# Right column halves of the first four row tiles by seven 256-column products, and a reordered dequantization, in a two-layer kernel on one core

## The chip, the cores and the metric

The kernel runs on one core of a Trainium2 chip. The time is the device time of one execution in microseconds (us); of several runs the median is given. The engines are TensorE (PE in the profile; its weight loads are PEld), VectorE (DVE), ScalarE (ACT), GpSimd (POOL) and SyncE (SP, which here only issues transfers). Each takes the instructions of its own queue in order and waits at an instruction until the semaphores that it needs have come.

## The reference

The input x has 2048 rows of 1024 (4 x 512). Two layers follow each other, each with a residual and a layer norm:

```python
attn = einsum('ds,td->st', w1, w2) * sparse_mask       # 1024 x 1024, nonzero near the diagonal
y = einsum('bds,st->bdt', x, attn) + b2
x = layernorm(x + gelu(y))

w = take_along_axis(lut4, idx, axis=1)   # 1024 x 1024; idx from 4 bit planes, 32 codes to an int32
x = layernorm(x + x @ w.T + bias)        # rows with a norm above 64 would use 8 bits
```

All of it is float32. In the data no row's norm exceeds the limit and the mask is zero outside its band; the kernel counts exceptions as it goes, and only if there were any would it run a general path.

## The kernel before

Rows are worked in 16 tiles of 128 (`NT`), features in 8 blocks of 128 (`KT`); `HALF` is 512 columns, which is one bank of TensorE's accumulators.

**Preparation.** `w2` is transposed block by block on TensorE, and the product with `w1` gives the band of `attn`, row block by row block (L454). VectorE multiplies each by its mask and so empties the bank (L476). Beside that the second layer's weight is dequantized (`dequantize_pair`). A pair is two blocks of 128 output features. Eight VectorE instructions (L297) spread the bits of the pair's codes into the tile `v`, of which there is one buffer. Each block has two sides. Each side has four entries, each a table value chosen by bit 0: three on ScalarE (L322) into one triple tile `e` (three buffers), one on GpSimd (L326) into `root`. VectorE's predicated copies (L329 to L331) choose between them by bits 1 and 2, and a last one (L335) between the sides by bit 3. The finished block is transposed on TensorE, and ScalarE copies it into `wT`. `steps(1)` in the code releases one further side of it after each row block and after some row tiles. The row tiles 2 to 11 are loaded when the preparation's memory is free, that is after the last L476.

**First layer.** `attention(n)` fills a bank pair with the bias (ScalarE, L526), adds ten matmuls (L532), takes the Gelu into `z` (two buffers), adds the residual with its row sum `total` (VectorE, L561), and calls `stats`. `stats` makes the negative mean `nm` (VectorE, L377), the sum of squares about it by a Square on ScalarE (L380), and on GpSimd the factor `r` (L382, L383). `normalize` (L387) is put off to a list, `later`, and issued by the next `now()`, after some of the following work.

**Second layer, row tiles 0 to 3 (`EARLY`).** The rows are transposed on TensorE into the tiles `kept`. Each tile has a left half of 512 columns, worked among the attentions 4 to 7, and a right half, worked among the attentions 12 to 15 (`SOON` is 12). A half is eight matmuls of 512 columns (L575) and one VectorE instruction that adds the bias and sums the row (`combine`, L587). After each right half comes one of the four weight sums (`weight_sum`, L636) that the pairs need.

**Second layer, row tiles 4 to 15, in pairs.** `ffn_pair` computes the two-by-two block product of a pair of row tiles in seven products of four matmuls of 512 columns instead of eight (L692). It needs four sums of weight blocks, t1 to t4, made once, and four of row blocks, s1 to s4, made for each pair (`pair_inputs`; s1 and s3 on VectorE L675, L676, s2 and s4 on GpSimd L678, L679). Its rows come transposed through memory: a VectorE transpose of 32 x 32 squares (`squares`, L642), a store to `there`, and four loads into `rows`. Three banks (u, v, w) hold partial products; VectorE reads u and w between products (L705, L709, L712), and a bank that is added to again must have been read first. The last row tile is finished in quarters (L762).

**Order of the work.** A scheduler orders each engine's queue, by its own estimates of when an instruction can start. From attention 8 on (`manual_schedule`) the VectorE queue has the order of the program instead. The outputs of the tiles 0 to 3 go through a tile `o` with one buffer.

Of the kernel before, what the change touches and what calls it, by code (L numbers as in the profile page):

```python
# [192 lines left out]
def kernel(  # L193
# [21 lines left out]
    with ExitStack() as main:  # L215
# [77 lines left out]
        def dequantize_pair(pair):  # L293

            v = dq.tile([P, 2 * B_L, 8, WORDS], I32, tag="v", name="v", bufs=1)
# [9 lines left out]
            bits = v.rearrange("o a s w -> o a (s w)").bitcast(U8)  # L305
            for t in range(2):
# [6 lines left out]
                for side in range(2):  # L313
                    e = dq.tile([P, 3, D], FP, tag="e", name="e", bufs=3)
                    root = dq.tile([P, D], FP, tag="root", name="root", bufs=4)
                    roots.append(root)
                    entry = [root, e[:, 0, :], e[:, 1, :], e[:, 2, :]]
# [14 lines left out]
                    if side == 0:  # L332
                        yield
# [19 lines left out]
        def dequantize_all():  # L353
            for pair in range(KT // 2):
                if pair == 1:
                    tc.keep_in_program_order(differences(2, KT))
                yield from dequantize_pair(pair)
# [7 lines left out]
        differences(0, 2)  # L365
        low = dequantize_all()
# [6 lines left out]
        def stats(u, total):  # L373
# [3 lines left out]
            nc.vector.tensor_scalar(nm, total, -1.0 / D, None, ALU.mult)  # L377
            junk = work.tile([P, D], BF, tag="junk", name="junk", bufs=1)
            ss = work.tile([P, 1], FP, tag="ss", name="ss", bufs=4)
            nc.scalar.activation(junk, u, AF.Square, bias=nm, accum_out=ss)  # L380
            r = work.tile([P, 1], FP, tag="r", name="r", bufs=4)
            nc.gpsimd.tensor_scalar(r, ss, 1.0 / D, EPS, ALU.mult, ALU.add)  # L382
# [200 lines left out]
        sums = const.tile([P, NT, NH], FP, name="sums")  # L583

        def combine(n, h, ps, other):

            return nc.vector.scalar_tensor_tensor(  # L587
                x_tiles[n][:, ts(h, HALF)],
# [5 lines left out]
                accum_out=sums[:, n, h : h + 1],  # L594
            )

        def finish_rows(n):
            y = x_tiles[n]
            total = work.tile([P, 1], FP, tag="total", name="total", bufs=4)
            nc.vector.tensor_tensor(total, sums[:, n, 0:1], sums[:, n, 1:2], ALU.add)  # L600
# [12 lines left out]
        def ffn_half(n, xT, h):  # L613
            ps = ps_mm.tile([P, D], FP, tag="mm", name="mm")
            product(ps[:, :HALF], xT, h)
            now()
            combine(n, h, ps[:, :HALF], bias_bc[:, ts(h, HALF)])
            if h == 1:
                finish_rows(n)
# [11 lines left out]
        def weight_sum(pool, i):  # L631
# [4 lines left out]
            nc.vector.tensor_tensor(weights[i], plus, minus, ALU.subtract)  # L636
# [21 lines left out]
        def pair_inputs(pool, n, top, low):  # L658
# [6 lines left out]
            def by_squares(block):  # L665
# [5 lines left out]
                halves(f"early{2 * i + side}") for i in range(3)  # L671
# [10 lines left out]
        def ffn_pair(pool, n, blocks, between):  # L682
# [6 lines left out]

            def times(ps, a, b, start, stop):  # L690
                for k in range(KH):
                    nc.tensor.matmul(  # L692
                        out=ps,
                        lhsT=a[:, k, :],
# [147 lines left out]
        for i, (what, n) in enumerate(todo):  # L842
# [14 lines left out]
            if what == "attention":  # L857
# [4 lines left out]
                if n < 2 * EARLY:  # L862
                    now()
# [63 lines left out]
```

## Time and profile before

| | |
|---|---|
| time, three runs | 360.46 us median (358.38 to 361.06) |
| time of the profiled execution | 360.45 us |
| its span | 358.7 us |
| busy | PE 92%, PEld 57%, DVE 60%, ACT 50%, POOL 25% |
| transfers | 43.90 MB, 122 GB/s over the span |
| mean granted TensorE clock | 0.973 |
| products of 512 columns in the pair stage, eight records | 3.43 us on the chain that ended last |
| a right half (L575, sixteen records) | 6.87 us on that chain |

A matmul on float32 appears as two records. The span runs from the first to the last instruction of the profiled execution, and the time of the same execution is 1.75 us longer. Busy shares are of the span. The profile's matmul durations overlap each other, so what a series costs is read from the starts of its records or from the chain, not from the mean of one.

### The profile page before, as it was taken

To read this page: it belongs to the slowest core of one execution; us is meant where nothing else is said; L and a number is where in the kernel's file an instruction comes from. 1 tells how busy PE (TensorE), PEld (TensorE's weight loads), DVE (VectorE), ACT (ScalarE), POOL (GpSimd) and SP (SyncE) were. 2 spreads that over 40 slices of the span, in tenths; PEclk is the share of its full clock that TensorE was granted. 3 is DMA by queue.
4 is the path that set the end of the run, shared out by engine and by line. 5 is a ranking of instruction groups with operands and counts; after the bars stand their busy time and mean duration, and the time that the engine had idled before them with its cause. 6 is when DMAs were issued, how large, how long until landed. Compare 5 with 4: busy or idle time off the path is not lost.

```text
span 358.7 us, 3719 instructions
## 1 busy us (share of the span) xinstructions
PE 329.9 (92%) x1228; PEld 205.7 (57%) x1228; DVE 214.5 (60%) x341; ACT 179.4 (50%) x257; POOL 90.9 (25%) x131
## 2 busy tenths in 40 slices
PE   7799867598999999999999998999999999999990
PEld 7688756495765759966656643443444443444450
DVE  0589898546997885436476853653644535634342
ACT  3795893978958988974346311303214114024020
POOL 1630431425013442312312530401304004004010
PEclk9899998879999999999999999999999999999996
DMA  8999207700000000320264425153554450441103
GB/s 250 320 320 384 80 0 288 298 2 0 0 0 2 1 0 3 126 111 26 79 215 165 140 80 175 58 199 100 199 177 137 188 175 8 189 154 58 58 3 125
DMA packets 28475, 43.90 MB, mean 122 GB/s; under 512 B 7584, under 2 KB 20640, under 8 KB 28448
## 3 DMA queue, kind: packets, MB, share of 16 engines
q1 hardware_dynamic: 26832, 42.66, 34.9%
q10 hardware_dynamic: 1616, 0.93, 0.9%
q8 instruction: 11, 0.18, 0.2%
q14 instruction: 16, 0.13, 0.1%
HBM read 28.90 MB, written 14.68 MB: 122 GB/s over the span
## 4 chain that ended last, share of the span: by engine, by line
PE 60%; ACT 12%; DMA 11%; DVE 8%; issue 3%; POOL 2%; SPq 2%; ACTq 0%; POOLq 0%; DVEq 0%
PE u L692 15%; PE mm L532 12%; PE mm L575 12%; PE w L692 8%; ACT e L322 6%; PE pt L281 5%; PE v L692 4%; PE mm L454 4%; DMA rows<-there 3%; ACT junk L380 2%; DMA q<-in_L_ffn_qweight_dram 2%; DMA x<-in_L_attn_x_dram 2%; DMA there<-squares 1%; DMA w_sb<-in_L_attn_w_dram 1%; SPq L652 1%
## 5 line engine op out<-in xcount | busy, mean ns | idle before, releaser
L532 PE MATMUL mm<-attn,xT 128*128 128x198 f32 (+2 forms) x320 | 62.5, 353 | 6.9 <-ACT mm L526 6.9
L380 ACT ACTIVATE junk<-x,nm 128x1024 bf16<-128x1024 f32 x31 | 35.7, 1151 | 59.7 <-DVE nm L377 57.3
L532 PEld LDWEIGHTS mm<-attn,xT 128*128 128x128 f32 x320 | 54.8, 197 | 14.6 <-ACT mm L526 7.6
L322 ACT ACTIVATE e<-v,lt,diff 128x1024 f32<-128x1024 uint8 x48 | 56.8, 1243 | 12.6 <-DVE v L297 11.0
L575 PE MATMUL mm<-wT,xT 128*128 128x512 f32 x128 | 56.4, 593 | 1.0 <-ACT wT L282 1.0
L326 POOL TENSOR_SCALAR root<-v,diff,lt 128x1024 f32<-128x1024 uint8 x16 | 31.3, 1965 | 57.9 <-DVE v L297 26.2
L692 PE MATMUL u<-t,halves 128*128 128x512 f32 x96 | 43.3, 593 | 1.0 <-DVE x L712 1.0
L575 PEld LDWEIGHTS mm<-wT,xT 128*128 128x128 f32 x128 | 23.7, 190 | 28.1 <-issue 26.1
L382 POOL TENSOR_SCALAR r<-ss 128x1 f32<-128x1 f32 x31 | 10.4, 334 | 108.8 <-ACT junk L380 108.6
L674 ACT COPY halves<-rows 128x1024 f32<-128x1024 f32 x6 | 6.3, 1048 | 55.4 <-DMA rows<-there 55.4
L454 PE MATMUL mm<-w2T,w_sb 128*128 128x268 f32 (+1 forms) x128 | 30.8, 391 | 2.2 <-ACT w2T L282 2.2
L692 PEld LDWEIGHTS u<-t,halves 128*128 128x128 f32 x96 | 18.2, 190 | 24.3 <-issue 22.5
L678 POOL TENSOR_TENSOR halves<-halves 128x512 f32<-128x512 f32 x6 | 9.5, 1585 | 84.5 <-DVE halves L675 68.3
L642 DVE STREAM_TRANSPOSE squares<-x 128x1024 f32<-128x1024 f32 x12 | 24.3, 2029 | 11.0 <-DMA there<-squares 11.0
L387 DVE TENSOR_SCALAR x<-x,nm,r 128x1024 f32<-128x1024 f32 x16 | 13.0, 813 | 29.0 <-POOL r L383 29.0
L330 DVE COPY_PREDICATED root<-v,e 128x1024 f32<-128x1024 uint8 x16 | 23.3, 1457 | 8.0 <-POOL root L326 4.6
L454 PEld LDWEIGHTS mm<-w2T,w_sb 128*128 128x128 f32 x128 | 23.8, 197 | 6.2 <-ACT w2T L282 2.7
L281 PE MATMUL pt<-ident,x 128*128 128x128 f32 x160 | 21.8, 281 | 4.0 <-DVE x L387 4.0
L561 DVE SCALAR_TENSOR_TENSOR x<-z,x 128x1024 f32<-128x1024 f32 x16 | 21.4, 1335 | 6.2 <-ACT z L557 6.2
L329 DVE COPY_PREDICATED e<-v,e 128x1024 f32<-128x1024 uint8 x16 | 21.3, 1329 | 3.5 <-ACT e L322 3.5
L281 PEld LDWEIGHTS pt<-ident,x 128*128 128x128 f32 x160 | 19.4, 152 | 5.9 <-DVE x L387 4.3
L282 ACT COPY xT<-pt 128x512 f32<-128x512 f32 x40 | 21.4, 591 | 2.3 <-PE pt L281 2.3
(93 smaller groups left out, 438.5 us busy)
## 6 DMA issues: line engine op xcount, KB each, us to landing
x<-in_L_attn_x_dram SPq DMA_DIRECT2D x16, 512.0 KB, 7.4
out_dram<-o SPq DMA_DIRECT2D x14, 512.0 KB, 2.6
there<-squares SPq DMA_DIRECT2D x12, 512.0 KB, 3.1
rows<-there SPq DMA_DIRECT2D x48, 128.0 KB, 2.9
w_raw<-in_L_attn_w_dram SPq DMA_DIRECT2D x8, 512.0 KB, 6.8
w_sb<-in_L_attn_w_dram SPq DMA_DIRECT2D x3, 1024.0 KB, 6.9
w_sb<-in_L_attn_w_dram SPq DMA_DIRECT2D x2, 512.0 KB, 7.2
x<-_L_attn_sparse_mask_dram SPq DMA_DIRECT2D x2, 413.0 KB, 3.7
```

The lines of the kernel that those rows point to most:

```text
L281: nc.tensor.transpose(pt[:, j, :], block(g * (HALF // P) + j), ident)
L282: done = nc.scalar.copy(dst[:, g * (HALF // P) : (g + 1) * (HALF // P), :], pt)
L322: nc.scalar.activation(entry[j], plane(0), AF.Identity, scale=d_k, bias=l_k)
L326: nc.gpsimd.tensor_scalar(entry[j], plane(0), d_k, l_k, ALU.mult, ALU.add)
L330: nc.vector.copy_predicated(root, plane(1), entry[1])
L380: nc.scalar.activation(junk, u, AF.Square, bias=nm, accum_out=ss)
L454: part = nc.tensor.matmul(out=ps[:, : hi - lo], lhsT=w1_sb[s][:, k, :], rhs=w2T[:, k, lo:hi], start=(k == 0), stop=(k == KT - 1),)
L532: nc.tensor.matmul(out=ps[:, a:b], lhsT=xT[:, s, :], rhs=attn[:, s, a - lo : b - lo], start=False, stop=hi == D or (h == 0 and window(s + ...
L561: nc.vector.scalar_tensor_tensor(xt, z, 1.0, xt, ALU.mult, ALU.add, accum_out=total)
L575: nc.tensor.matmul(out=ps, lhsT=xT[:, k, :], rhs=wT[:, k, ts(h, HALF)], start=(k == 0), stop=(k == KT - 1),)
L642: nc.vector.transpose(out=t, in_=x_tiles[n].rearrange("t (c j k) -> t c k j", c=Q, k=KT))
L692: nc.tensor.matmul(out=ps, lhsT=a[:, k, :], rhs=b[:, k, :], start=start and k == 0, stop=stop and k == KH - 1, skip_group_check=True,)
```

## The change

**The first right halves.** The row tiles 0 to 3 are taken by twos. `early_blocks` makes the four sums of row blocks for two tiles (two on VectorE, two on GpSimd); it is called for both twos after attention 10. `right_weight_sums` makes four sums of 512 x 256 weight blocks on VectorE after attention 11. `ffn_rights` computes the two right halves in seven products of four matmuls with 256 columns; its banks u and w are taken from the transposes' banks, v from the main ones. It is called twice, ahead of attentions 12 and 14. Each row's sum now has three parts. The weight sums for the pairs stand after the attentions 12, 14 (two) and 15, and numbers 1 and 3 run on GpSimd. The first two `squares` come after the attentions 12 and 13 instead of 13 and 14.

**The dequantization.** `v` has two buffers, and a pair's bits are spread (`unpack`) in the middle of the second block of the pair before. The entries have single buffers, seven of them, instead of three triples.

**The statistics.** The Square takes the row's sum as its bias and -1024 as its scale, so that its result is larger by 1024 x 1024, which `r` and the count of exceptions take out again. `nm` is made on GpSimd.

```diff
-            v = dq.tile([P, 2 * B_L, 8, WORDS], I32, tag="v", name="v", bufs=1)
+        def unpack(pair):
+            v = dq.tile([P, 2 * B_L, 8, WORDS], I32, tag="v", name="v", bufs=2)
...
-                    e = dq.tile([P, 3, D], FP, tag="e", name="e", bufs=3)
...
-                    entry = [root, e[:, 0, :], e[:, 1, :], e[:, 2, :]]
+                    entry = [root] + [
+                        dq.tile([P, D], FP, tag="e", name="e", bufs=7) for _ in range(3)
+                    ]
...
                     if side == 0:
+                        if t == 1 and pair + 1 < KT // 2:
+                            if pair == 0:
+                                tc.keep_in_program_order(differences(2, KT))
+                            unpack(pair + 1)
                         yield
...
-            nc.vector.tensor_scalar(nm, total, -1.0 / D, None, ALU.mult)
+            nc.gpsimd.tensor_scalar(nm, total, -1.0 / D, None, ALU.mult)
...
-            nc.scalar.activation(junk, u, AF.Square, bias=nm, accum_out=ss)
+            nc.scalar.activation(junk, u, AF.Square, scale=float(-D), bias=total, accum_out=ss)
...
-            nc.gpsimd.tensor_scalar(r, ss, 1.0 / D, EPS, ALU.mult, ALU.add)
+            nc.gpsimd.tensor_scalar(r, ss, 1.0 / D**3, EPS, ALU.mult, ALU.add)
...
-            nc.vector.tensor_tensor(weights[i], plus, minus, ALU.subtract)
+            engine = nc.gpsimd if i % 2 else nc.vector
+            engine.tensor_tensor(weights[i], plus, minus, ALU.subtract)
...
+        def right_weight_sums(pool):
...
+            nc.vector.tensor_tensor(t1, r12, r11, ALU.subtract)
+            nc.vector.tensor_tensor(t2, r22, t1, ALU.subtract)
+            nc.vector.tensor_tensor(t3, r22, r12, ALU.subtract)
+            nc.vector.tensor_tensor(t4, r21, t2, ALU.subtract)
...
+        def early_blocks(pool, n):
+            a11, a12 = kept[n][:, :KH, :], kept[n][:, KH:, :]
+            a21, a22 = kept[n + 1][:, :KH, :], kept[n + 1][:, KH:, :]
...
+            nc.vector.tensor_tensor(s1, a21, a22, ALU.add)
+            nc.vector.tensor_tensor(a21, a11, a21, ALU.subtract)
+            nc.gpsimd.tensor_tensor(s2, s1, a11, ALU.subtract)
+            nc.gpsimd.tensor_tensor(s4, a12, s2, ALU.subtract)
...
+        def ffn_rights(n):
...
+            times(u, a11, r11, True, False)
+            nc.vector.tensor_tensor(y11, u, left, ALU.add)
+            times(w, s1, t1, True, False)
+            nc.vector.tensor_tensor(y22, w, right, ALU.add)
+            times(u, s2, t2, False, False)
+            nc.vector.tensor_tensor(y12, u, right, ALU.add)
+            times(w, s4, r22, False, True)
+            combine(n, 3, w, y12, R)
+            times(u, s3, t3, False, False)
+            combine(n + 1, 3, u, y22, R)
+            now()
+            times(v, a12, r21, True, True)
+            combine(n, 2, v, y11, R)
+            finish_rows(n)
+            times(u, a22, t4, False, True)
+            combine(n + 1, 2, u, left, R)
+            now()
+            finish_rows(n + 1)
...
-        for m in range(EARLY):
-            todo += [("right", m), ("attention", SOON + m)]
+        for m in range(0, EARLY, PAIR):
+            todo += [("rights", m), ("attention", SOON + m), ("attention", SOON + m + 1)]
...
-                if n >= SOON + 1:
-                    attention(n, xT, lambda: prepare_pair(EARLY, n - SOON - 1))
+                if SOON <= n <= SOON + PAIR:
+                    attention(n, xT, lambda: prepare_pair(EARLY, n - SOON))
...
+                if n == SOON - 2:
+                    for m in range(0, EARLY, PAIR):
+                        early_blocks(last, m)
+                if n == SOON - 1:
+                    now()
+                    right_weight_sums(last)
+                for i in {SOON: (1,), SOON + 2: (2, 3), SOON + 3: (4,)}.get(n, ()):
+                    weight_sum(last, i)
+            elif what == "left":
+                ffn_left(n, xT)
             else:
-                ffn_half(n, xT, 0 if what == "left" else 1)
-                if what == "right":
-                    weight_sum(last, n + 1)
-                    now()
+                ffn_rights(n)
```

## Prediction

> **What bounds the kernel now.** I read the page's engine rows first, then busy time by stretch, then TensorE's timeline.
>
> ```profile
> span 358.7 us, 3719 instructions
> PE 329.9 (92%) x1228; PEld 205.7 (57%) x1228; DVE 214.5 (60%) x341; ACT 179.4 (50%) x257; POOL 90.9 (25%) x131
> ```
>
> ```profile
> 50.70:92.50 41.80, 31.23 (x146) 25.18 (x146) 28.49 (x40) 32.13 (x43) 16.19 (x21) 0.88 0.32 126
> 92.50:149.00 56.50, 55.08 (x282) 41.04 (x281) 44.77 (x66) 48.68 (x65) 16.79 (x24) 1.00 0.00 1
> 149.00:201.50 52.50, 52.50 (x218) 35.33 (x217) 30.71 (x47) 28.03 (x42) 13.75 (x31) 1.00 0.39 134
> 201.50:227.40 25.90, 24.56 (x58) 10.50 (x57) 14.87 (x22) 4.91 (x7) 8.03 (x9) 1.00 0.35 116
> 227.40:350.30 122.90, 121.14 (x291) 54.37 (x289) 58.53 (x110) 28.88 (x59) 20.34 (x32) 1.00 0.36 126
> ```
>
> The first figure after the length of a stretch is PE's busy time. Only 50.7 to 92.5 leaves it much idle; 149.0 to 201.5, which the change rewrites, has no gap at all. TensorE is the bound, and what any other engine does counts where TensorE must wait for it. Its timeline shows those places (in brackets the wait and its releaser):
>
> ```profile
> 14.72 3.76 PE L454 MATMUL mm<-w2T,w_sb 128*128 128x268 f32 x8 [2.02 <-ACT w2T L282]
> ...
> 56.24 5.33 PE L532 MATMUL mm<-attn,xT 128*128 128x198 f32 x20 [5.49 <-ACT mm L526]
> ...
> 70.96 1.97 PE L281 MATMUL pt<-ident,x 128*128 128x128 f32 x8 [4.04 <-DVE x L387]
> ...
> 85.49 7.13 PE L575 MATMUL mm<-wT,xT 128*128 128x512 f32 x16 [1.03 <-ACT wT L282]
> ...
> 212.33 3.67 PE L692 MATMUL w<-wT,halves 128*128 128x512 f32 x8 [0.34 <-DVE x L709]
> 217.00 3.70 PE L692 MATMUL u<-t,halves 128*128 128x512 f32 x8 [1.00 <-DVE x L712]
> ...
> 249.05 3.67 PE L692 MATMUL u<-t,a 128*128 128x512 f32 x8 [0.88 <-ACT a L677]
> ```
>
> A wait also costs clock. By stretches again, PEclk third from last:
>
> ```profile
> 14.70:18.40 3.70, 3.68 (x9) 2.70 (x10) 2.12 (x3) 3.70 (x4) 3.70 (x3) 0.54 1.22 329
> 56.20:61.40 5.20, 5.16 (x20) 4.55 (x21) 5.10 (x7) 0.94 (x1) 0.00 (x0) 0.71 0.95 375
> 70.90:74.40 3.50, 3.44 (x16) 3.45 (x17) 3.50 (x6) 3.13 (x5) 0.05 (x1) 0.50 0.00 0
> ```
>
> After waits of 2.0, 5.5 and 4.0 us the clock is 0.54, 0.71 and 0.50 for some 4 us, while the waits of about 1 us kept 1.00. I charge 1.7 us (half of 3.5) after a long wait, and half of that, 0.9, after one of 2 to 3.5 us.
>
> **The change, part by part** (times on the old kernel's clock until I shift them).
>
> *Seven products instead of eight halves.* In the chain eight records (four fp32 matmuls) of 512 columns take 3.43 us and a right half, sixteen, 6.87; eight records of 256 columns (L762) take 1.73. So 4 x 6.87 = 27.5 becomes 14 x 1.72 = 24.1: -3.4 us, all on the path. Were weight loads the limit, a product could not fall below 8 x 0.19 = 1.52, so they are not; 1.72 is measured.
>
> *Bits and entries.* Eight extractions (1.72 us) of a pair move ahead of the end of the pair before. Now ScalarE waits for them three times, 11.0 us in all, the longest 6.1. In the built order the vector queue meets the second pair's first extraction at about 20.1, where the codes have not landed: SP issues them up to 17.9, landing takes 5.8, so it stands until some 23 with predicated copies and mask products behind it (TensorE needs the held product bank only at 25.5, so it doesn't wait). The bits are then ready at 33.4 instead of 37.7. ScalarE follows with entries at 1.17 us each and its copies, and its first bias copy (L526) ends at 53.2 instead of 56.1: -3. The built order then puts attentions 2 and 3 ahead of the first left product, where TensorE now waits 4.04 us for x0 and runs at half clock: 53.2, two attentions of 3.6 with their 0.87 transposes to 63, attention 2 to 66.6 (x0 is ready at 66.4), attention 3 to 71.1, transposes to 73.8. The left product needs four wT copies that stand behind a Gelu and two Squares on ScalarE: 77.3 against 85.49, -8.2; the wait of 3.5 us ahead of it costs 1.7 of clock. Net -6.5. Seven single entries instead of nine in triples hold ScalarE back only if it runs more than seven ahead; I find it there once, by less than 1 us. Bounds: 0 (the later vector queue eats it all) to -15 (all that TensorE loses between 50.7 and 85.5 in waits and slow clock); I stay at the walked value. After that the dequantization has slack: the last root is built at 137.3 and transposed at 146.2.
>
> *Square on the row's sum.* Each statistic loses nm (0.15 us on DVE and its hand-over) ahead of the Square; POOL gains 31 x 0.19 = 5.9 us beside 75% idle time. Worth about 0.25 us a chain; counted in the walk below.
>
> *The added vector and POOL work around the right products.* The vector engine follows program order from attention 8 on. New in it: four block sums of 512 (0.69 each), four weight sums of 1024 (half of L636's 2.28: 1.15 each), fourteen bank reads of 256 instead of four of 512. On POOL: s2 and s4 twice (L678 1.59, L679 1.27), and weight sums 1 and 3 of 2048. No row shows the latter: from below two one-input 1024s, 2 x 1.20 = 2.4; from above 4 x 1.59 = 6.4; nearest is 4 x 1.27 less three fixed parts of 0.19: 4.5.
>
> Where they stand decides. POOL's queue has weight sum 1 between nm and r of row tile 9, so r comes at 154.8 instead of 151.4, and normalizing x9 heads the vector queue: the residual of tile 10 moves from 153.8 to 155.6, the four block sums end at 159.4, and s2, s4 stand ahead of r of tile 10 on POOL (normalized at 161.5), again of tile 11 (167.0). The first right weight sum ends at 168.9. TensorE has the first and last products and six matmuls of attention 12 to do, until about 163, and then waits for it: +5.8 us, and 1.7 of clock. Bounds: 3 (weight sum 1 free) to 9.
>
> Second: the output tile "o" has one buffer, and two stores (2.6 us each) now follow each other instead of 11 us apart. Behind the last bank read at 182: Square and r, o(0), the store, o(1), a 1.95 stream transpose, a residual, its statistic, another transpose, another residual, 15.4 us until the second pair's first bank is read, beside 12.9 of TensorE work: +2.5 and 0.9 of clock. Third: the same two stores of the second pair, two halves, two residuals, weight sums 2 and 4 (2.28 each) stand ahead of the first 512 pair's bank read: +3.1 and 0.9. That pair loses its old waits (-1.7) and gains one of 0.9 on u, since v is used up earlier; the pair behind it has v to fill its wait: -1.0. Bounds of these two waits together: 0 to 10.
>
> Sum: -6.5 - 3.4 + 7.5 + 3.4 + 4.0 - 1.7 + 0.9 - 1.0 = +3.2, a span of 361.9. The profiled execution took 360.45 around a span of 358.7, so 1.75 is added: **363.6 us**. Its 360.45 is also the median of the runs (360.46).
>
> The Trainium skill (TensorE: Matmul & The Clock Gate, Part 1) states that the clock falls to half after an idle window of about 3.4 us. The row at 14.72 shows 0.54 after only 2.02 us. By the page alone the waits of 2.5 and 3.1 us would cost no clock and the time would be 361.8.
>
> **Rivals.**
> *The vector engine keeps up.* The first wait is only its lower bound of 3.0, without slow clock, and the other two vanish: -6.5 - 3.4 + 3.0 - 1.7 + 0.9 - 1.0 = -8.7, **351.8 us**. For it: DVE is busy only 31 of 52.5 us there. Against: it is the order, not the load, that makes it late. It decides from the point where the three waits and their clock come to less than 8 us instead of 14.9.
> *No early gain.* If the codes land later, or contention slows the predicated copies (1.2 us alone, up to 2.23 beside POOL's roots), the first left product starts as late as before and only the middle counts: 363.6 + 6.5 = **370.1**; half of it gives 366.9.
> *The products don't shrink*: 256 columns at their 379 ns record instead of 215: 112 x 0.164 = 18 us more. L762 in the chain speaks against it.
>
> **How the numbers follow.** The walk as it stands 0.43, the vector engine keeping up 0.31, no or half an early gain 0.24, no shrinking 0.02. About 1% (3.6 us) is what a measurement can tell from no change. Faster by over 1%: the second case, 0.31. The forecast lies 0.9% above the old time and splits into 0.27 within and the rest above; with the other slow cases 0.42 slower. The likeliest case has its own range, 360 to 368. The range for 8 in 10 goes from 352 to 369.5.
>
> **What would show it.** Right: the first left product near 77; TensorE waiting for a vector weight sum for about 6 us after attention 11; two waits of 2 to 4 us for vector bank reads, one before attention 15 and one in the first 512 pair; the stretch from attention 11 to the last attention longer than before although its products are shorter. Wrong: the first left product near 85; no wait of TensorE above 3 us after attention 11; r of tile 9 not behind POOL's weight sum; 256-column products of more than 1.8 us.

## The result, and the profile after

The kernel after takes **373.46 us** (median of four runs, 372.06 to 375.58) against 359.55 us before: ratio 1.0389, 95% interval 1.0321 to 1.0458. It is slower, as the likeliest case said, but by 13.9 us, not by 3: the time lies above the range. The profiled execution took 375.58 us, its span is 15.1 us longer than that of before.

The page's first rows, after:

```profile
span 373.8 us, 3831 instructions
PE 331.3 (89%) x1275; PEld 214.9 (57%) x1276; DVE 216.2 (58%) x330; ACT 178.8 (48%) x257; POOL 138.4 (37%) x168
```

TensorE is busy for about as long as before (329.9 us) in a longer span; POOL has 47 us more. Busy time by stretch, cut where the same work begins: the first left product, attention 10, the first 512 pair, the second 512 pair, the end of TensorE's work (columns as in the prediction: behind the length of the stretch PE's busy time, then that of PEld, DVE, ACT and POOL; the clock is third from last).

```profile
0.00:80.01 80.01, 65.78 (x370) 57.55 (x371) 58.17 (x92) 62.14 (x79) 38.32 (x29) 0.98 0.66 218
80.01:144.04 64.03, 62.27 (x299) 44.08 (x297) 47.24 (x55) 54.60 (x72) 34.22 (x40) 1.00 0.00 1
144.04:210.17 66.13, 55.65 (x267) 48.05 (x265) 30.07 (x52) 26.13 (x39) 28.03 (x41) 0.90 0.26 92
210.17:243.00 32.83, 26.26 (x58) 11.18 (x58) 20.44 (x22) 6.66 (x10) 11.95 (x15) 0.95 0.36 120
243.00:365.40 122.40, 121.35 (x291) 54.06 (x289) 57.96 (x104) 29.27 (x59) 25.36 (x44) 1.00 0.36 127
```

Before, the same five took 85.49, 63.48, 52.55, 25.88 and 122.90 us. So the first one gained 5.5 us, the third (which holds the rewritten right halves) lost 13.6 and the first 512 pair 7.0; the others moved by 0.5 us each. TensorE's timeline has the places:

```profile
52.94 3.86 PE L542 MATMUL mm<-attn,xT 128*128 128x198 f32 x20 [2.63 <-ACT mm L536]
71.05 1.12 PE L281 MATMUL pt<-ident,x 128*128 128x128 f32 x8 [3.35 <-DVE x L397]
80.01 7.13 PE L585 MATMUL mm<-wT,xT 128*128 128x512 f32 x16
...
165.11 3.78 PE L690 MATMUL w<-t,halves 128*128 128x256 f32 x8 [5.87 <-DVE t L667]
171.95 1.89 PE L690 MATMUL u<-t,halves 128*128 128x256 f32 x8
173.68 1.89 PE L690 MATMUL w<-wT,s 128*128 128x256 f32 x8
197.24 3.75 PE L690 MATMUL u<-t,halves 128*128 128x256 f32 x8 [4.42 <-DVE x L715]
226.32 5.15 PE L690 MATMUL u<-t,halves 128*128 128x512 f32 x8 [5.69 <-DVE x L789]
239.34 3.67 PE L690 MATMUL u<-t,a 128*128 128x512 f32 x8 [0.88 <-DVE x L598]
```

The three waits that were forecast are there, and at their places: the first right weight sum after attention 11, the second group's bank read, the first 512 pair's bank read. At full clock a 256-column product takes 1.73 us (171.95 to 173.68). Behind the first two waits it takes twice that, and the 512-column product behind the third takes 5.0 us instead of 3.43 (226.32 to 231.31). The clock in the stretches behind the three waits shows why:

```profile
165.10:172.00 6.90, 6.89 (x24) 5.83 (x25) 4.24 (x5) 1.29 (x3) 0.00 (x0) 0.55 0.00 0
197.20:203.20 6.00, 5.96 (x17) 4.91 (x18) 0.65 (x2) 3.81 (x5) 3.28 (x5) 0.60 0.40 128
226.30:231.40 5.10, 5.08 (x9) 2.35 (x10) 3.32 (x3) 0.00 (x0) 1.02 (x3) 0.71 0.23 96
```

6.9 x 0.45 + 6.0 x 0.40 + 5.1 x 0.29 = 7.0 us of clock, where 3.5 were charged. What the vector engine stood for, in its own timeline (in brackets its wait):

```profile
150.03 0.81 DVE L397 TENSOR_SCALAR x<-x,nm,r 128x1024 f32<-128x1024 f32 x1 [6.01 <-POOL r L393]
163.10 0.81 DVE L397 TENSOR_SCALAR x<-x,nm,r 128x1024 f32<-128x1024 f32 x1 [3.73 <-POOL r L393]
163.83 1.22 DVE L667 TENSOR_TENSOR t<-wT 128x1024 f32<-128x1024 f32 x1
186.72 0.81 DVE L397 TENSOR_SCALAR o<-x,nm,r 128x1024 f32<-128x1024 f32 x1 [5.24 <-DMA out_dram<-o]
212.87 0.81 DVE L397 TENSOR_SCALAR o<-x,nm,r 128x1024 f32<-128x1024 f32 x1 [2.96 <-DMA out_dram<-o]
```

and on POOL, why r of row tile 9 came late: the weight sum stands between `nm` and r.

```profile
144.11 0.22 POOL L387 TENSOR_SCALAR nm<-total 128x1 f32<-128x1 f32 x1 [1.18 <-DVE x L571]
144.52 4.54 POOL L650 TENSOR_TENSOR t<-wT 128x2048 f32<-128x2048 f32 x1 [0.19 <-issue]
149.15 0.19 POOL L392 TENSOR_SCALAR r<-ss 128x1 f32<-128x1 f32 x1
```

The waits and their clock are 5.87 + 4.42 + 5.69 + 7.0 = 23.0 us, more than the whole loss of 15.1 us of span, beside which stand the early gain and the shorter products. The vector queue in program order is full of instructions that wait for something, while the engine itself is busy 30 of the 66 us of the third stretch.

### The profile page after: what moved, and what is told of

Same layout as the page of the kernel before. It is cut to its first block, busy times and chain, and to the rows that moved or that the text cites. A ratio compares the mean times of both kernels' runs of the same rounds, so it can differ in the third digit from the quotient of the medians.

```text
span 373.8 us, 3831 instructions
## 1 busy us (share of the span) xinstructions
PE 331.3 (89%) x1275; PEld 214.9 (57%) x1276; DVE 216.2 (58%) x330; ACT 178.8 (48%) x257; POOL 138.4 (37%) x168
## 4 chain that ended last, share of the span: by engine, by line
PE 43%; DVE 19%; POOL 15%; DMA 9%; issue 5%; ACT 4%; SPq 3%; POOLq 0%; DVEq 0%; ACTq 0%
PE u L690 14%; PE w L690 8%; PE mm L585 6%; PE mm L542 6%; PE pt L281 4%; POOL root L333 4%; PE v L690 3%; DMA rows<-there 3%; DVE squares L737 3%; DVE e L336 3%; DVE root L338 2%; ACT junk L390 2%; POOL r L393 2%; DMA out_dram<-o 2%; DMA there<-squares 2%
## 5 line engine op out<-in xcount | busy, mean ns | idle before, releaser
L390 ACT ACTIVATE junk<-x,total 128x1024 bf16<-128x1024 f32 x31 | 35.7, 1152 | 77.8 <-DVE x L571 34.0
L333 POOL TENSOR_SCALAR root<-v,diff,lt 128x1024 f32<-128x1024 uint8 x16 | 49.1, 3076 | 43.0 <-DVE root L346 17.6
L690 PE MATMUL u<-t,halves 128*128 128x512 f32 (+1 forms) x112 | 50.6, 598 | 10.2 <-DVE x L789 5.7
L690 PEld LDWEIGHTS u<-t,halves 128*128 128x128 f32 x112 | 22.6, 206 | 35.9 <-issue 21.9
L387 POOL TENSOR_SCALAR nm<-total 128x1 f32<-128x1 f32 x31 | 15.5, 500 | 72.4 <-DVE x L571 33.7
L690 PE MATMUL w<-t,halves 128*128 128x512 f32 (+1 forms) x64 | 27.2, 573 | 5.9 <-DVE t L667 5.9
L464 PE MATMUL mm<-w2T,w_sb 128*128 128x268 f32 (+1 forms) x128 | 29.2, 376 | 2.9 <-ACT w2T L282 2.8
L585 PE MATMUL mm<-wT,xT 128*128 128x512 f32 x64 | 28.4, 596 | 1.8 <-DVE x L598 1.8
L337 DVE COPY_PREDICATED root<-v,e 128x1024 f32<-128x1024 uint8 x16 | 21.1, 1320 | 5.5 <-POOL root L333 5.5
L690 PEld LDWEIGHTS w<-t,halves 128*128 128x128 f32 x64 | 13.2, 208 | 18.5 <-issue 11.5
```

What stands on the lines that cost most here:

```text
L333: nc.gpsimd.tensor_scalar(entry[j], plane(0), d_k, l_k, ALU.mult, ALU.add)
L337: nc.vector.copy_predicated(root, plane(1), entry[1])
L390: nc.scalar.activation(junk, u, AF.Square, scale=float(-D), bias=total, accum_out=ss)
L464: part = nc.tensor.matmul(out=ps[:, : hi - lo], lhsT=w1_sb[s][:, k, :], rhs=w2T[:, k, lo:hi], start=(k == 0), stop=(k == KT - 1),)
L585: nc.tensor.matmul(out=ps, lhsT=xT[:, k, :], rhs=wT[:, k, ts(h, HALF)], start=(k == 0), stop=(k == KT - 1),)
L690: done = nc.tensor.matmul(out=ps, lhsT=a[:, k, :], rhs=b[:, k, :], start=start and k == 0, stop=stop and k == KH - 1, skip_group_check=True,)
```

## The experiments

Each time is beside runs of the kernel before on the same chip. "Middle" is the profiled time from the first left product to the second 512 pair, which holds all that the change lost. `e_...` names a run.

| kernel | us (median) | ratio to before, 95% | first left product | middle |
|---|---|---|---|---|
| before | 359.55 | | 85.49 | 141.9 |
| after | 373.46 | 1.0389 (1.0321-1.0458) | 80.01 | 162.8 |
| `after_again` | 373.60 | 1.0398 (1.0360-1.0436) | 79.92 | 161.3 |
| `e_old_rights` | 354.96 | 0.9892 (0.9848-0.9935) | 80.97 | 142.6 |
| `e_new_rights` | 378.77 | 1.0557 (1.0482-1.0631) | 85.45 | 160.7 |
| `e_deq_only` | 357.23 | 0.9939 (0.9916-0.9961) | 82.41 | 143.0 |
| `e_sums_first` | 370.55 | 1.0335 (1.0288-1.0381) | 79.81 | 156.7 |
| `e_sums_later` | 370.41 | 1.0297 (1.0248-1.0345) | 80.28 | 158.3 |
| `e_o_two` | 372.56 | 1.0386 (1.0337-1.0435) | 79.91 | 158.0 |
| `e_nm_vector` | 372.25 | 1.0357 (1.0320-1.0395) | 79.51 | 161.2 |
| `e_wsum_vector` | 374.24 | 1.0412 (1.0371-1.0453) | 80.05 | 162.0 |
| `e_no_sums` | 358.31 | 0.9963 (0.9932-0.9994) | 80.02 | 143.5 |
| `e_order_pool` | 370.47 | 1.0304 (1.0258-1.0350) | 81.76 | 155.1 |
| `e_order_vector` | 352.98 | 0.9822 (0.9782-0.9861) | 79.81 | 140.9 |
| `e_order_again` | 353.76 | 0.9842 (0.9805-0.9878) | 79.85 | 141.5 |
| `e_mix_blocks` | 353.59 | 0.9830 (0.9787-0.9872) | 80.21 | 141.7 |
| `e_mix_weights` | 356.04 | 0.9886 (0.9838-0.9933) | 79.84 | 144.3 |
| `e_one_o` | 359.14 | 0.9999 (0.9980-1.0018) | 79.82 | 144.0 |
| `e_lump` | 360.63 | 1.0026 (1.0005-1.0046) | 80.00 | 145.7 |
| `e_apart` | 354.53 | 0.9856 (0.9827-0.9886) | 80.54 | 139.4 |

### The parts of the change, one at a time

`e_old_rights` is before with the new dequantization and statistics; `e_new_rights` is before with everything else of the change.

> The kernel before with the new dequantization and the new statistics, but with the old right halves, two to a pair of row tiles and 512 columns wide. In the profile after, the early stretch (to the first left product) is 5.5 us shorter than before, the next stretch 0.5 longer, and the whole loss lies behind: 13.6 us from attention 10 to the first 512 pair, 7.0 in that pair. Theory A: the loss belongs to the seven products and to the order of the work that feeds them, so this kernel keeps the early gain alone: 354 to 356 us, 4 to 5.5 below before. Rival B: the loss belongs to the statistics, whose sign change now runs on POOL and there takes up to 2.2 us beside vector work: then the pairs of 512 lose here too, and the time is 361 or more.

> The kernel before with the seven products, their block and weight sums and their order, but with the old dequantization and the old statistics. Theory A: the middle and the first 512 pair lose what they lose in the kernel after, 17 to 21 us: 377 to 381 us. Rival B (the statistics on POOL are half of it): 366 to 371 us. Rival C (the two parts hurt only together): within 3 us of before.

354.96 and 378.77: theory A in both. The dequantization and the statistics together are a gain of 1.1%, and the seven products with their order of work lose 20 us by themselves, with the old statistics as well.

### Removing one suspect from the kernel after

`e_sums_first` puts the right weight sums ahead; `e_sums_later` in addition leaves out the line that normalizes tile 11 there (comment added):

```diff
                 if n == SOON - 2:
+                    right_weight_sums(last)
                     for m in range(0, EARLY, PAIR):
                         early_blocks(last, m)
                 if n == SOON - 1:
                     now()                # e_sums_later: both lines gone
-                    right_weight_sums(last)
```

> The kernel after, with the four right weight sums put ahead of the block sums, at attention 10, not behind the normalization of row tile 11. Theory: it is the order of the vector queue that makes TensorE wait 5.9 us for the first sum (it ended at 165.1, behind 3.7 us in which the vector engine waited for r of tile 11) and then run at half clock; with the sums first that wait and some 2 to 3 us of slow clock go, 6 to 9 us in all: 364.5 to 367.5. Rival: the vector engine has too much to do there, and the wait moves to the block sums or to the bank reads: less than 2 us saved.

The first wait shrank from 5.9 to 1.3 us, and the time falls by only 3 us: the next bank read is late in its place, with the same slow clock, and the third wait grew from 5.7 to 6.4. TensorE, `e_sums_first`:

```profile
155.61 1.99 PE L690 MATMUL w<-t,halves 128*128 128x256 f32 x8 [1.33 <-DVE halves L682]
167.11 3.75 PE L690 MATMUL u<-t,halves 128*128 128x256 f32 x8 [5.03 <-DVE x L715]
```

> As the run with the right weight sums first, and the normalization of row tile 11 isn't called for ahead of the first product's bank read any more, so that the vector queue doesn't wait for r of that tile there (2.3 us). With the sums first the wait for the first sum went (5.9 to 1.3 us) and one of 5.0 us came two products later, for that bank read. Theory: the vector queue's order sets each of these waits; this one falls from 5.0 to below 2 us and the time to 364 to 367. Rival (the vector engine has more to do there than TensorE whatever the order): the wait only moves on, and the time stays at 369 or more.

370.41: the rival's number, a miss for the theory. That wait fell from 5.0 to 4.3 only, because the vector engine still waited 6.0 us for r of tile 9 behind POOL's weight sum, and the sums stood behind that.

`e_o_two` lets the odd row tiles be normalized in place, so that two stores never share the buffer:

```diff
-                    o = last.tile([P, D], FP, tag="o", name="o")
+                    o = y if n % 2 else last.tile([P, D], FP, tag="o", name="o")
```

> The kernel after, but the normalized rows of tiles 1 and 3 are written in place and stored from there, so that no two stores share the one output buffer. Theory: the vector engine stood 5.24 us (tile 1) and 2.96 us (tile 3) for the store of the tile before; the second wait of TensorE (4.4 us and 2.5 of slow clock) goes, and the third (5.7 and 1.5) shrinks by about 3: 7 to 10 us in all, 363.5 to 366.5. Rival: without the stores the vector engine meets the next late thing (r of POOL, the Square) and TensorE's waits shrink by less than a third: 371 or more.

The second wait fell from 4.4 to 1.3 us and the middle by 3.4 against `after_again`, yet the ratio didn't move beyond its interval. In its profile the pairs behind the middle take 124.8 us where the kernel after has 122.4: TensorE's queue there was ordered differently, with waits of 0.4 to 1.0 us for bank reads in some of the pairs. That happened in several runs below and goes with some 2 to 3 us each time.

`e_nm_vector` puts `nm` back on the vector engine, `e_wsum_vector` the weight sums 1 and 3.

> The kernel after once more, on the same chip and against the same runs as the three kernels beside it, since the differences to it are of 1 to 8 us: 371 to 375 us. Its waits stand where they stood: for the first right weight sum 5.9 us, for the second pair's bank read 4.4, for the first 512 pair's 5.7.

> The kernel after with the sign change of the row sum back on the vector engine; the Square still takes the row's sum. Theory (order of the vector queue): the sign change on POOL costs the pairs little, since TensorE's long waits were as long in the kernel that had the old statistics with the seven products (5.5, 4.3, 5.7 us): 0 to 2 us less than after. Rival: the sign changes of 2.2 us beside the sums of the weights on the vector engine make the third wait, which falls below 3.5 us: 3 us or more less than after.

> The kernel after with weight sums 1 and 3 of the 512 pairs back on the vector engine. Theory: POOL's weight sum of 4.5 us, which its scheduler put between the sign change and r of row tile 9, makes the vector engine wait 6.0 us there, and with it the block sums and the first right weight sum; without it TensorE's first wait falls from 5.9 to 2 to 4 us, while the vector engine has 2 x 2.28 us more to do behind it, so the second or third wait grows by about as much: 371 to 374 us in all. Rival (POOL's sums cost the vector engine nothing): the first wait stays at 5.9 us and the time rises to 375 or more.

Against 373.6 for the kernel after again, `nm` is worth 1.4 us (the intervals overlap). With the weight sums on the vector engine the first wait fell from 5.9 to 4.5 and the third grew from 5.7 to 7.6: nothing gained.

So each suspect, taken away alone, gives 0 to 3 us of 20. Two readings were left: too much work, or work in the wrong order and place.

### Work or order

> The kernel after without any of the sums that the products of sums and differences need: neither the four right weight sums and the block sums nor the four weight sums of the 512 pairs are made, raw slices stand in their place. All products, bank reads, stores, statistics and transposes remain. Theory (making the operands is what the vector queue has no time for): the first and the third long wait go with their clock, some of the second (4.4 us, the store of the one output buffer ahead of it) stays; early gain 5.5 and products 3.4 remain: 350 to 357 us. Rival (bank reads, stores and the statistics' chains alone make the vector queue late): waits of over 8 us remain, 361 or more.

358.31: between theory and rival. This kernel leaves the sums out, so it doesn't compute the layer; it only shows what the rest costs. The long waits are gone (the longest in the middle is 2.1 us, at full clock), but of the 8.9 us that the early gain and the shorter products should give only 1.5 are left in its profile. The early 5.5 arrive. The middle takes 143.5 us, 1.6 more than before although its products are 3.4 shorter: the statistics' chains of 2.3 us and stores of 3.0 still stand in the vector queue ahead of the bank reads. The later pairs, ordered differently again, lose 2.4.

`e_order_pool` was the first try at another order.

> The kernel after with its work put in another order, nothing left out: right weight sums first, no normalization of tile 11 ahead of the bank reads, both groups of seven products with one attention between them (the stream transposes, weight sums and inputs of the first 512 pair behind them), odd tiles' rows written in place, the fourth weight sum inside the first 512 pair, and POOL's instructions in program order from attention 8 on, so that its weight sum doesn't come ahead of r of tile 9. Theory: all three long waits are matters of order, and what is left is the early gain (5.5), the shorter products (3.4) and 1 to 5 us of waits: 351 to 357 us. Rival: the seven products need more vector and POOL work than TensorE's time there covers; waits of over 3 us remain and the time is 360 or more, no better than the old right halves with the new dequantization (355).

The rival's number. It showed something else: the two engines hold each other up. Vector timeline first, then POOL's:

```profile
208.97 4.98 DVE L397 TENSOR_SCALAR x<-x,nm,r 128x1024 f32<-128x1024 f32 x1 [2.29 <-ACT halves L769]
```

```profile
208.91 4.50 POOL L650 TENSOR_TENSOR t<-wT 128x2048 f32<-128x2048 f32 x1
```

A normalization that takes 0.81 us elsewhere took 4.98, as long as POOL's sum of 4.50 ran beside it. Its stream transposes came too late as well, and TensorE stood 6.3 us at the first 512 pair for the rows. So the next order has all sums of this stretch on the vector engine, cut small, in the gaps between bank reads (comments added):

```diff
+        todo += [("rights", 0), ("attention", SOON), ("rights", PAIR)]
+        todo += [("attention", n) for n in range(SOON + 1, NT)]
...
             times(u, a11, r11, True, False)
             nc.vector.tensor_tensor(y11, u, left, ALU.add)
             times(w, s1, t1, True, False)
             nc.vector.tensor_tensor(y22, w, right, ALU.add)
+            fill(0)       # first group: right sum 3, s1 of the second group, right sum 4, ...
             times(u, s2, t2, False, False)      # second group: weight sums 1 and 2 in halves
             nc.vector.tensor_tensor(y12, u, right, ALU.add)
+            fill(1)
...
-            nc.gpsimd.tensor_tensor(s2, s1, a11, ALU.subtract)
+                lambda: nc.vector.tensor_tensor(s2, s1, a11, ALU.subtract),
...
+            if n == EARLY:                      # in the first 512 pair, behind y22's read
+                for f in weight_sum(last, 4):
+                    f()
```

The right sums 1 and 2 stand between attention 10's residual and its normalization, the first group's block sums behind that, the stream transposes behind each group's last read, `nm` on the vector engine, and the odd tiles in place.

> The seven products in a third order, nothing left out: all block sums, right weight sums, weight sums and sign changes on the vector engine (POOL keeps roots and r until the 512 pairs), cut in pieces of 0.7 to 1.2 us and put into the gaps of about 1.3 us between the bank reads; stream transposes of the first 512 pair behind each group's last read; odd tiles' rows written in place; the fourth weight sum inside the first 512 pair. In the run before this (POOL in program order) vector work of 0.69 to 1.22 us took 1.6 to 2.3 beside POOL's block sums, and one normalization took 4.98 instead of 0.81 beside POOL's weight sum of 4.50. Theory (order and the two engines' getting in each other's way): waits of 2 to 6 us in all remain: 351 to 357 us. Rival (too much vector work for TensorE's time there, whatever the order): 360 or more.

> The reordered kernel once more beside it, in five rounds, as the version that beats both kernels: 352 to 354 us, 1.4 to 2.1% below before; no wait of TensorE above 2.6 us, as in its first profile.

352.98 and 353.76: **faster than both kernels**, with the same products and every sum made. It is 1.8 and 1.6% below before (both intervals end below 1, neither proves 2%) and 20 us below the kernel after. TensorE's waits in the middle:

```profile
118.23 7.11 PE L585 MATMUL mm<-wT,xT 128*128 128x512 f32 x16 [0.63 <-DVE x L598]
153.14 1.97 PE L697 MATMUL w<-t,halves 128*128 128x256 f32 x8 [0.77 <-DVE halves L689]
171.91 1.99 PE L697 MATMUL u<-t,halves 128*128 128x256 f32 x8 [0.24 <-DVE x L722]
205.42 3.67 PE L697 MATMUL w<-wT,halves 128*128 128x512 f32 x8 [1.14 <-DVE x L804]
210.29 3.70 PE L697 MATMUL u<-t,halves 128*128 128x512 f32 x8 [1.19 <-DVE x L810]
```

None of these costs clock. From the first left product to the first 512 pair it takes 113.4 us; before took 116.0, so 2.6 of the 3.4 us that the shorter products save arrive there, with 1.6 us of waits (its first three above). The first 512 pair, which now holds the fourth weight sum, takes 27.5 us instead of 25.9 and gives 1.6 of that back. Against `e_old_rights` (354.96), which has the early gain without the seven products, 352.98 and 353.76 are 1 to 2 us less, and the intervals overlap: what the seven products are worth in the end is small and not settled. The vector engine in the part from the first 256-column product to the first 512 pair (its busy time is 34.72, behind the length, PE and PEld):

```profile
150.48:193.18 42.70, 41.69 (x218) 36.87 (x217) 34.72 (x68) 21.28 (x32) 10.79 (x24) 1.00 0.41 132
```

It is busy 34.7 of 42.7 us, where the kernel after used 27.7 of 57.8: there was time enough.

This order differs from the kernel after in three things at once: the places in the queues, the engine of the sums and signs, and the odd tiles' output.

### What of the order carries it

Each of five runs puts one thing back into this order. `e_mix_blocks`: s2 and s4 on POOL. `e_mix_weights`: weight sums 1 and 3 on POOL. `e_one_o`: one output buffer. `e_lump`: the sums out of the gaps, ahead of each group. `e_apart`: the second group behind two attentions again.

> The reordered kernel with all sums on the vector engine (353.0 us), with one thing put back as the kernel after has it: the second and fourth block sum of each group (four of 512 columns) on POOL. Theory A (the two engines slow each other): each takes 1.3 to 1.8 us on POOL, the vector engine's work of two inputs beside it doubles, and r stands behind them: 2 to 6 us more, 355 to 359. Theory B (only the place in the vector queue matters): it has 2.8 us less to do, and the time stays within 1.5 us of 353.0 or falls.

> The reordered kernel with weight sums 1 and 3 of the 512 pairs put back on POOL, each in two pieces of 1024. TensorE's order is unchanged. Theory A: about 9 us of POOL beside the vector engine, with r behind it: 2 to 6 us more, 355 to 359. Theory B: the vector engine has 4.6 us less to do and the time stays within 1.5 us of 353.0 or falls.

> The reordered kernel with the one output buffer for all four row tiles again, none written in place. Theory A (the wait for the store decides wherever it stands in the vector queue): the vector engine stands 3 to 5 us twice, TensorE waits 2 to 4 us once or twice and loses clock: 355 to 360. Theory B (with little else in the queue there the stall is absorbed): within 1.5 us of 353.0.

> The reordered kernel, with the sums that stand in the gaps between the bank reads pulled out of them: two right weight sums and the second group's block sums (2 x 1.22 + 4 x 0.69 = 5.2 us) all ahead of the first group's first bank read, four pieces of weight sums (4.6 us) all ahead of the second group's. Same engines, same instructions. Theory A (the place in the vector queue decides, the gaps are the gain): each group's third product waits 2 to 4 us for its bank read and loses clock: 357 to 363. Theory B (with the store wait and POOL's sums gone the queue has room, and TensorE's order adapts): within 1.5 us of 353.0.

> The reordered kernel with the second group of seven products back where the kernel after has it, behind two attentions and not one; everything else, its sums in the gaps too, as in the reordered kernel. Theory A (the statistics' chain of attention 12, 2.3 us, and the residual of attention 13 now stand ahead of the second group's first bank read, and the second stream transpose comes later, close to the first 512 pair): TensorE waits 2 to 4 us in one or both places: 356 to 361 us. Theory B (place of the group doesn't matter once its sums are in the gaps): within 1.5 us of 353.4.

Block sums on POOL cost nothing measurable (+0.6), though they took up to 2.14 us there: the gaps absorb it. The group's place costs 1.1 us or less, and what it costs lies in the later pairs (124.8 us instead of 122.1), while its middle of 139.4 us is the shortest of all. POOL's weight sums cost 3.1 us against the first run of the reordered kernel and 2.3 against the second. The vector engine waits for r of tile 9 again, and TensorE's first wait is followed by a clock of 0.61 for 4 us (`e_mix_weights`):

```profile
148.36 0.81 DVE L397 TENSOR_SCALAR x<-x,nm,r 128x1024 f32<-128x1024 f32 x1 [5.49 <-POOL r L393]
155.18 2.87 PE L697 MATMUL w<-t,halves 128*128 128x256 f32 x8 [2.28 <-DVE halves L689]
```

The one buffer costs 6.2 us (5.4 against the second run), of which the middle shows 3.2 and the later pairs 2.4. In `e_one_o` the vector engine stands for both stores, and TensorE waits once, with the clock at 0.57 for 4 us:

```profile
173.23 0.81 DVE L397 TENSOR_SCALAR o<-x,nm,r 128x1024 f32<-128x1024 f32 x1 [3.81 <-DMA out_dram<-o]
191.72 0.81 DVE L397 TENSOR_SCALAR o<-x,nm,r 128x1024 f32<-128x1024 f32 x1 [4.07 <-DMA out_dram<-o]
202.55 5.40 PE L697 MATMUL w<-t,halves 128*128 128x512 f32 x8 [2.32 <-DVE halves L781]
```

The lump costs 6.9 us against the reordered kernel beside it, 4.2 of it in the middle, but not as theory A said: no wait exceeds 1.8 us, TensorE's queue was ordered anew around the late reads, and the loss is spread over many small waits. Singly these come to 15 to 18 us of the 20, though part of it is the later pairs' order (2.4 to 2.6 in `e_one_o` and `e_lump`). In the kernel after they stand behind each other in one queue, which would explain why removing one there gave so little; how they share the loss when together was not shown run by run.

### The early stretch

> The kernel before with the new dequantization alone (bits of the next pair unpacked early in two buffers, single entry buffers), old statistics, old right halves. With the new statistics as well the time was 355.0. Theory: in the early stretch the sign change on POOL stood behind a root of 4.8 us and held the normalization of row tile 0 (at 70.1 where 66.4 was worked out), so without it the first left product comes 1 to 3 us sooner, at 77 to 79: 352 to 354.5 us. Rival: r is on POOL anyway and waits behind the same roots, so the sign change costs nothing: 355 to 356.5.

357.23: the theory was the wrong way round, and the time is above the rival's range as well. Without the new statistics the first left product comes later, 82.41 against 80.97. TensorE in `e_deq_only`:

```profile
72.31 1.94 PE L281 MATMUL pt<-ident,x 128*128 128x128 f32 x8 [3.53 <-DVE nm L387]
```

There row tile 0 waits for `nm` as well, behind predicated copies on the vector engine; in `e_old_rights` the same transposes start at 72.01, 0.3 us sooner. The other 1.1 us stand behind them, where attention 3 ran at a lower clock in the one profile than in the other (5.78 against 4.75 us); two profiles can't tell that from chance. So the new statistics as a whole don't delay row tile 0. `e_nm_vector`, which has the new Square with `nm` on the vector engine, starts these transposes at 70.47, the kernel after at 71.05 and 71.03 in its two profiles: `nm` on POOL costs about 0.6 us there, not the 1 to 3 of the theory. Whether the statistics bring something (0.9892 against 0.9939, with intervals that overlap) was not settled.

## Why the prediction was right and wrong

**Right.** The direction and its reason. The places of all three waits and what releases them. The first wait, 5.8 forecast and 5.87 measured, with what starts its chain (r of tile 9 behind POOL's weight sum: 4.5 forecast, 4.54 measured). That it agrees so closely is in part luck: counted from attention 10, the right weight sum and TensorE's stop before it both came 1.1 to 1.2 us later than in the walk. And POOL's sum is only one link: without it (`e_wsum_vector`) 4.5 us of the wait stayed, and only the order of `e_sums_first` took it to 1.3. The product of 256 columns: 1.72 and 1.73. The first bias copy: 53.2 forecast, TensorE starts on it at 52.94. The waits behind the first 512 pair's u: 0.9 and 0.88.

**The early gain** was -6.5 and is -5.5. The walk's step from 53.2 to 63 is 0.9 us more than the parts that it names; the two attentions with their transposes ended at 63.94. The step that failed is row tile 0, ready at 66.4 in the walk and normalized at 70.1. On POOL a root of 4.76 us stands ahead of its `nm` and r:

```profile
62.82 4.76 POOL L333 TENSOR_SCALAR root<-v,diff,lt 128x1024 f32<-128x1024 uint8 x1 [4.01 <-DVE root L346]
67.66 1.46 POOL L387 TENSOR_SCALAR nm<-total 128x1 f32<-128x1 f32 x1
69.21 0.19 POOL L392 TENSOR_SCALAR r<-ss 128x1 f32<-128x1 f32 x1
```

A root takes 1.20 us where it is shortest; the 16 roots took 3.08 us each instead of the 1.97 of before. That they are slow because, with bits that are there early, more of them run beside predicated copies fits the rows, but no run separates it. Contention was listed as a rival, with the copies as the slow ones; it was worth 1 us, not 6.5.

**The second and third wait** were mis-sized: 2.5 became 4.4, and 3.1 became 5.7, together 10.1, just above the 10 that the forecast gave as their bound. In the second, the store was taken at 2.6 us, the median of stores; the vector engine stood 5.24 for the first store (4.42 to 5.24 in four other profiles with the one buffer, 2.97 to 2.99 in three) and 2.96 for the third. SP issues a load of the mask 0.45 us behind each of the two; whether that slows a store, and why the first mostly takes so much longer than the third, was not settled. In the third wait, vector work took longer beside POOL. Vector timeline, then POOL's:

```profile
214.80 2.29 DVE L571 SCALAR_TENSOR_TENSOR x<-z,x 128x1024 f32<-128x1024 f32 x1
217.02 3.35 DVE L650 TENSOR_TENSOR t<-wT,t 128x2048 f32<-128x2048 f32 x1
```

```profile
214.36 1.65 POOL L773 TENSOR_TENSOR halves<-halves 128x512 f32<-128x512 f32 x1 [2.17 <-DVE halves L770]
216.09 2.13 POOL L774 TENSOR_TENSOR halves<-halves 128x512 f32<-128x512 f32 x1
218.30 2.15 POOL L387 TENSOR_SCALAR nm<-total 128x1 f32<-128x1 f32 x1
```

The residual took 2.29 instead of 1.22 and weight sum 2 took 3.35 instead of 2.28, which makes 2.1 of the 2.6 us by which this wait grew. POOL's `nm` took 2.15 and 2.20 instead of the 0.19 that the forecast put "beside 75% idle time", but that isn't what makes the wait: with `nm` on the vector engine it was 5.79 (`e_nm_vector`) and 5.71 (`e_new_rights`). The walk had contention as a rival for the early stretch only.

**The clock** was the largest single error: 1.7 + 0.9 + 0.9 = 3.5 charged, 7.0 measured. Half price for a wait of 2 to 3.5 us was no bad mean: a wait of 2.50 to 2.63 us ahead of attention 0 stands in seventeen of the profiles here, and in six the clock behind it stayed at 1.00, in eleven it fell to 0.57 to 0.67 for 4 us, among them two profiles of one and the same kernel (`e_order_vector`, 2.54 us: 1.00; `e_order_again`, 2.55 us: 0.58). The loss over the seventeen is 1.0 us in the mean, where 0.9 was charged. But the second and third wait grew out of that class, and the full price is 1.5 to 3.1 us: in the middle of the kernels every wait of 3.8 us or more cost it, and waits of 1.72, 1.83 and 2.12 us cost nothing. The Trainium skill (TensorE: Matmul & The Clock Gate, Part 1) has the clock fall after an idle window of about 3.4 us, and says that this window runs freely, so that it depends on where in it the work lands. The chance at 2.5 us agrees with a free-running window; that waits of 2.3 to 2.6 us were enough at all doesn't agree with its length, and there the measurement decides.

**The old waits** of the first pairs were to give 1.8 us and gave 0.8.

Together: waits two and three 4.5, clock 3.5, early 1.0, old waits 1.0, and 0.5 in the stretch of the left products make 10.5 of the 11.9 us by which the sum was low; 1.4 us stay unassigned.

**The rivals.** "The vector engine keeps up" (351.8) is not this kernel, but its argument held: the vector engine's load was not the limit. `e_order_vector`, with all of that load and more of it on the vector engine, takes 353.0. "No early gain" and "no shrinking" fell. The forecast's own sentence, that it is the order and not the load that makes the engine late, was the finding. The steps that failed are sizes in its sum: it priced the order by single rows as if each instruction ran alone (waits two and three, 5.6 charged and 10.1 measured), and charged half the clock that such waits cost (3.5 and 7.0).

## What to carry to other kernels

An engine whose queue is written by hand is late by the sum of all waits in front of the instruction that matters, not by its load: price each wait at what it will be beside its neighbours, and expect that removing one uncovers the next. Put preparatory work into the gaps that the consumer's own rhythm leaves, in pieces as short as those gaps, and nothing that waits for a transfer or another engine in front of a bank read. In the middle of these kernels a wait of TensorE of about 4 us and more cost another 1.5 to 3 us in clock and one of 2 us nothing, so two short waits were cheaper than one long one of the same sum.

## What the runs showed of the hardware that I had not expected

- An instruction on POOL can hold one of the vector engine until it is done itself. The normalization of 0.81 us took 4.98 beside a sum of 4.50, although it has one input; this is one row. Two-input vector work shows the same in the rows above: POOL's block sum ran until 218.22, and weight sum 2, begun at 217.02, ended 2.15 us behind it, which is about its own length of 2.28. So what it loses is what the other still had to run. Not all vector work is held: beside POOL's weight sum of 4.52 in the kernel after (from 201.07) two bank reads (203.31 and 205.04) kept their 0.42 us. The Trainium skill (GPSIMD Engine Reference, Key points) names this contention for vector instructions with two inputs or in a mode that uses both ports; how long the hold lasts is from the rows.
- Tiny POOL instructions suffer too: `nm` on 128 x 1 took up to 2.20 us beside vector work, against 0.22 alone. The one of 2.15 us ended at 220.45, 0.08 behind the vector engine's weight sum.
- Between 2.0 and 2.6 us waits that look alike did and didn't cost TensorE's clock: 2.28 and 2.32 us gave 0.61 and 0.57, 2.29 us in `e_deq_only` kept 1.00, some 2.5 us gave 1.00 six times and 0.57 to 0.67 eleven times. For attention 0 that is up to 1.7 us, though the next wait can swallow it: the two profiles of the reordered kernel, one of each sort, have their first left product at 79.81 and 79.85.
- Changing the order in one place changed the order that the scheduler chose for TensorE in pairs far behind it, which went with 2.4 to 2.8 us. A difference of that size between two orders says nothing about the place that was edited.
